# One tile of every fifth group fetched by SP, row by row, in a graph-network layer on one Trainium2 core

## The chip, the cores and the metric

The kernel runs on one core of one Trainium2 chip. The core has five engines that run their own instruction streams and meet through semaphores: TensorE (PE in the profile, with its weight loads shown as PEld), VectorE (DVE), ScalarE (ACT), GpSimd (POOL) and SyncE (SP), which computes nothing and issues transfers. Sixteen DMA engines move data between the chip's memory and the core's on-chip memory. SP and ACT issue transfers that hardware turns into descriptors; POOL issues gathers whose descriptors it makes itself, from a list of row numbers.

The metric is the device time of one execution in microseconds (us), as the median of several runs. A profiled execution gives the span from the first to the last instruction, and a record of each instruction.

## The reference

The kernel computes one layer of a graph network on 12500 nodes of 256 features, with 200000 edges sorted by destination. All is float32.

```python
h = jnp.maximum(_layernorm(x, axis=-1), 0.0)
agg = segment_sum(h[src], dst, num_segments=N)      # 200000 rows gathered and added up by node
z = (1.0 + eps_gin) * h + agg
t = relu(batchnorm(z @ W1 + b1, g1, bt1))           # 256 -> 512, statistics over all nodes
out = relu(batchnorm(t @ W2 + b2 + h, g2, bt2))     # 512 -> 256, statistics over all nodes
return x + out
```

The gather `h[src]` reads 200000 rows of 1 KB. Since a batch normalisation needs the statistics of all nodes, the kernel has three stages: everything up to `z @ W1`, then W2, then the output.

## The kernel before

**Tiles and groups.** The edges are cut into 1563 tiles of 128 edges (the last has 64), the tiles into 131 groups of 12 (`GT`). The nodes are cut into 25 chunks of 512. `srcT` holds the source node numbers, one column a tile; a gather of one tile fetches 128 rows, one to a partition.

**The first stage** is one loop over rounds i = 0 to 134 in `fast()` (L307), under `tc.manual_schedule()`: on each engine the instructions stand in the order in which the Python code records them. A round has, in this order:

- `gather(i + 4)` (L429): POOL issues 12 indirect transfers, tile 11 of the group first and tile 0 last, into the buffer of that group. There are five such buffers (`AHEAD + 1`), so a buffer is used again five groups later, once PE has read it. For the groups up to 29 (`LEAD`) the rows come from `x` and are normalised after landing (`settle`, L363); from group 30 on they come from `h_tab`, the table of normalised rows that the kernel itself wrote in rounds 0 to 24.
- `add` (L501) on DVE adds an earlier group's result into the chunk's accumulator `zc`.
- `take` (L522), when a slice is ready: DVE takes statistics (L525), ACT copies the slice to `ts` (L527) and stores it to `t_tab` (L528). A chunk has four slices, so there are about three `take`s in four rounds.
- `hold` (L483): ACT copies the sum of group i - 2 out of PSUM (`zs`, L485). `edges` (L460): DVE builds the selection matrices `oh` of group i + 1.
- `sums(i)` (L471): PE multiplies the 12 tiles by their selection matrices (L478), tile 0 first, and adds them up in one PSUM tile. Float32 matmuls appear as two records each, 24 to a group.
- `put(i - 2)` (L491): PE places the group's 128 sums at their nodes (L496).
- `z_load(c)` (L451): SP loads a chunk's `zc` start value from `h_cols` (four buffers); two rounds later `z_scale` (L458) on ACT scales it. `slice_of` (L509): PE computes one slice of `z @ W1` (L514).

**The second stage** loops over the chunks: SP loads `t_tab` (L626, three buffers) and `h_cols` (L627), ACT normalises (L630), PE multiplies by W2 (L637), DVE adds and takes statistics (L641, L642). **The third** normalises, transposes back, adds `x` and stores (L657 to L668). The order of these two is made by the framework's scheduler.

**Transfers and their counters.** The framework gives transfers that SP and ACT issue eight landing semaphores in turn, and a transfer waits until the one before it on the same semaphore has landed. POOL's gathers have eight of their own.

Of the kernel before, what the change touches and what calls it, by code (L numbers as in the profile page):

```python
# [6 lines left out]

F32 = mybir.dt.float32
I32 = mybir.dt.int32
AF = mybir.ActivationFunctionType  # L10
OP = mybir.AluOpType
PSUM = bass.MemoryType.PSUM
# [2 lines left out]
P = 128  # L15
R = 4
EPS = 1e-5
GT = 12
MARGIN = 64
AHEAD = 4  # L20
LEAD = 30
EARLY = 2
LOW = 8
XAHEAD = 10
XMORE = 6

# [7 lines left out]
def kernel(  # L34
# [16 lines left out]
    nc = tc.nc  # L51
    N, D = x.shape
# [9 lines left out]
    for g in range(NCH):  # L62
        rows = min(CH, N - g * CH)
# [9 lines left out]
    NG = -(-NTILE // GT)  # L73
# [7 lines left out]
    h_tab = dram.tile([N, D], F32, name="h_tab")  # L81

    def move(eng, sb, table, g, store):
# [13 lines left out]

    jp = consts.tile([P, P], I32, name="jp")
    nc.gpsimd.iota(jp, pattern=[[1, P]], base=0, channel_multiplier=-1)
# [6 lines left out]

    srcT = consts.tile([P, NBLK * P], I32, name="srcT")
    dstT = consts.tile([P, NBLK * P], F32, name="dstT")
    shift = consts.tile([P, NG], F32, name="shift")
    base = consts.tile([P, NG], F32, name="base")  # L110
    flag = consts.tile([1, 1], I32, name="flag")
    col_i = consts.tile([P, WIDE], I32, name="col_i")
    row_i = consts.tile([P, 1], I32, name="row_i")
    srcE = consts.tile([P, EARLY * GT], I32, name="srcE")
    lands = [
        (consts.tile([P, LOW, D], F32, name=f"gta{k}"), consts.tile([P, GT - LOW, D], F32, name=f"gtb{k}"))
        for k in range(EARLY)
    ]

    def slot(ga, t):  # L120

        if len(ga) == 1:
            return ga[0][:, t, :]
        return ga[0][:, t, :] if t < LOW else ga[1][:, t - LOW, :]

# [18 lines left out]
    at = 0  # L144
# [6 lines left out]
    with ExitStack() as es:  # L151
# [15 lines left out]
        with tc.issue_after(placed.ins):  # L167
# [35 lines left out]
            pb, lhsT=first, rhs=dstT[:, : NG * GT].rearrange("p (g t) -> p g t", t=GT)[:, :, 0],  # L203
            start=True, stop=True,
# [16 lines left out]
        below = raw.tile([P, NG * GT], F32, name="below")  # L221
# [11 lines left out]
        for k, (v, t0, rows, n, e) in enumerate(checks):  # L233
            nc.scalar.activation(
                below[:rows, :n], v[:rows, t0 : t0 + n], AF.Relu, bias=zero[:rows], scale=-1.0,
                accum_out=cnt[:rows, 2 * k : 2 * k + 1],
# [4 lines left out]
                op0=OP.add, op1=OP.max,  # L241
# [12 lines left out]
        at = 0  # L254
# [15 lines left out]
    def norm(pool, st, mv, count, gamma, beta, bias, tag):  # L270
# [6 lines left out]
        mean = pool.tile([P, count], F32, name="mean" + tag)  # L277
        nc.scalar.activation(sd, mv[:, :, 1], AF.Sqrt, bias=epst)
        nc.vector.reciprocal(sc, sd)
# [7 lines left out]
    def layernorm(ln, xt, w, ht):  # L287
# [6 lines left out]
        sd = ln.tile([P, R], F32, name="sd")  # L294
        nc.scalar.activation(sd[:w], mv[:w, :, 1], AF.Sqrt, bias=epst[:w])
        rs = ln.tile([P, R], F32, name="rs")
# [5 lines left out]
        for c in range(R):  # L302
            nc.scalar.activation(
                ht[:w, c, :], xt[:w, c, :], AF.Relu, bias=nb[:w, c : c + 1], scale=rs[:w, c : c + 1]
            )

    def fast():  # L307

        parts = []
        for n0, w in chunks:  # L310
            n = w * R
# [20 lines left out]
        with ExitStack() as fs:  # L332
            keep = fs.enter_context(tc.tile_pool(name="keep", bufs=1))
# [7 lines left out]
            with ExitStack() as es:  # L341
                ln = es.enter_context(tc.tile_pool(name="ln", bufs=2))
                gat = es.enter_context(tc.tile_pool(name="gat", bufs=AHEAD + 1 - EARLY))
                sel = es.enter_context(tc.tile_pool(name="sel", bufs=2))
# [18 lines left out]
                def settle(v, pairs, rows, to, tag):  # L363
# [4 lines left out]
                    for c in reversed(range(0, n, 2)):  # L368
                        two = v[0][:, c : c + 2, :] if len(v) == 1 or c < LOW else v[1][:, c - LOW : c - LOW + 2, :]
                        nc.vector.bn_stats(  # L370
# [3 lines left out]
                    sd = sel.tile([P, n], F32, name="sd" + tag)  # L374
                    nc.scalar.activation(sd, st[:, :, 2], AF.Sqrt, bias=epst, scale=1.0 / D)
                    rs = sel.tile([P, n], F32, name="rs" + tag)
# [3 lines left out]
                    for c in reversed(range(rows)):  # L380
                        nc.scalar.activation(  # L381
                            slot(to, c), slot(v, c), AF.Relu, bias=nb[:, c : c + 1], scale=rs[:, c : c + 1]
                        )

                xts, hts, pcs = {}, {}, {}

                def x_chunk(g):
# [41 lines left out]
                def gather(i):  # L429
                    t0, n = groups[i]  # L430
                    k = i % (AHEAD + 1)
                    ga = lands[k] if k < EARLY else (gat.tile([P, GT, D], F32, name="gt"),)
                    for t in reversed(range(t0, t0 + n)):
                        rows = left if t == full_tiles else P
                        nc.gpsimd.indirect_dma_start(  # L435
                            out=slot(ga, t - t0)[:rows], out_offset=None, in_=x if i < LEAD else h_tab,
                            in_offset=bass.IndirectOffsetOnAxis(ap=srcT[:rows, t : t + 1], axis=0),
                        )
                    gathered[i] = ga
# [31 lines left out]
                def sums(i):  # L471

                    t0, n = groups[i]
                    ga, oh = gathered.pop(i), ohs.pop(i)
                    ps = ps_s.tile([P, D], F32, name="ps")
                    for j in range(n):
                        rows = left if t0 + j == full_tiles else P
                        nc.tensor.matmul(  # L478
                            ps, lhsT=oh[:rows, j, :], rhs=slot(ga, j)[:rows], start=(j == 0), stop=(j == n - 1)
                        )  # L480
                    summed[i] = ps

# [47 lines left out]
                def first(c):  # L530

                    return min(i for i in range(NG) if c in reach(i))
# [6 lines left out]
                for i in range(EARLY, min(AHEAD, NG)):  # L539
                    gather(i)  # L540
# [3 lines left out]
                for c in range(NCH):  # L544
                    k = max(first(c) + 1, c + 2)
# [4 lines left out]
                for i in range(NG + 4):  # L550
                    before = added
                    if i + AHEAD < NG:
                        gather(i + AHEAD)

                    late = 4 if i < NG else 3
                    while added <= min(i - late, NG - 1):
                        add(added)
                        added += 1
                    for c, f in taken:
                        take(c, f)  # L560
                    taken = []
                    if 0 <= i - 2 < NG:
                        spots(i - 2)
                        hold(i - 2)
                    if i + 1 < NG:
                        edges(i + 1)

                    if i < NCH:
                        h_chunk(i)
                    if i + 1 < min(LEAD, NG):  # L570
                        settle(gathered[i + 1], GT // 2, GT, gathered[i + 1], "g")
                    for c in scales.get(i, ()):
                        z_scale(c)

                    if i < NG:
                        sums(i)
                    if 0 < i <= NCH:
                        turn(i - 1)
                        turn_out(i - 1)
                    if 0 <= i - 2 < NG:  # L580
                        put(i - 2)
                    for c in loads.get(i, ()):
                        z_load(c)
                    while whole < NCH and last(whole) < (before if i < NG else added):
                        queue += [(whole, f) for f in range(HC)]
                        whole += 1
                    if i < NG:
                        some = queue[:1]
                    else:
                        some = queue  # L590
                    queue = queue[len(some):]
                    if i < NG:
                        for c, f in some:
                            slice_of(c, f)
                        taken = some
                    else:
                        for c, f in some:
                            slice_of(c, f)
                            take(c, f)
# [7 lines left out]

            xin = fs.enter_context(tc.tile_pool(name="xin", bufs=XAHEAD - EARLY, reuse_waits="tile"))
            xrs = []

            def x_rows(g):
                if g < NCH:
                    if XAHEAD - EARLY <= g < XAHEAD:
                        xrs.append(lands[g - XAHEAD + EARLY][1])
                    else:
                        pool = xmore if XAHEAD <= g < XAHEAD + XMORE else xin
                        xrs.append(pool.tile([P, R, D], F32, name="xr"))
# [3 lines left out]
            with tc.tile_pool(name="tin", bufs=3, side="right", reuse_waits="tile") as tin, tc.tile_pool(name="ps_y", bufs=4, space=PSUM) as ps_y:  # L621

                for k, g in enumerate([*range(NCH - 2), NCH - 1, NCH - 2]):
                    n = chunks[g][1] * R
# [9 lines left out]
                    for d in range(DC):  # L634
                        py = ps_y.tile([P, CH], F32, name="py")
                        for f in range(HC):
                            nc.tensor.matmul(  # L637
                                py[:, :n], lhsT=w2s[:, f, d * P : (d + 1) * P], rhs=tT[:, f, :n],
                                start=(f == 0), stop=(f == HC - 1),
                            )  # L640
                        nc.vector.tensor_add(yT[g][:, d, :], py[:, :n], yT[g][:, d, :])  # L641
                        nc.vector.bn_stats(st2[:, d, g, :], yT[g][:, d, :])  # L642
                for g in range(XAHEAD):
                    x_rows(g)
# [4 lines left out]
            with tc.tile_pool(name="xmore", bufs=XMORE, side="right", reuse_waits="tile") as xmore, tc.tile_pool(  # L649
                name="ps_o", bufs=3, space=PSUM  # L650
            ) as ps_o:
                for g in range(XAHEAD, XAHEAD + XMORE):
                    x_rows(g)
# [270 lines left out]
```

## Time and profile before

| | us |
|---|---|
| median of 3 runs (lowest to highest) | 2235.57 (2233.42 to 2241.05) |
| the profiled execution's own time | 2235.88 |
| its span | 2233.7 |
| POOL's last gather ends at | 1959.3 |
| PE's last matmul of L478 ends at | 1970.9 |

| engine | busy us | share of the span |
|---|---|---|
| PE | 1478.6 | 66% |
| POOL | 1480.4 | 66% |
| DVE | 716.5 | 32% |
| ACT | 510.1 | 23% |

How to read the profile: busy time does not count the instructions that only issue a transfer, wait, branch or load a register, so SP has no busy time at all and its issues are listed under SPq (ACT's under ACTq). A line such as `1204.72 0.94 POOL L435 DMA_INDIRECT gt<-h_tab,srcT x1 [0.30 <-issue]` is the start, the duration, the engine, the source line, the operation, what is written and read, how many instructions are merged, and in brackets how long the engine sat idle before it and what ended that; "issue" means that it waited for nothing that the profile shows. In the windows by engine the columns are PE, PEld, DVE, ACT and POOL, each with busy time and number of instructions. DMA shares are means over 16 engines. The five gather buffers are named gt, gta and gtb (two are split in two).

### The profile page before, as it was taken

How to read it: one execution, taken by the hardware profiler on the slowest of the kernel's cores; microseconds unless marked ns; L12 is line 12 of the kernel's file. 1: busy time of each engine (PE TensorE's matmuls, PEld its weight loads, DVE VectorE, ACT ScalarE, POOL GpSimd, SP SyncE). 2: the span in 40 equal slices, each digit the busy share in tenths (PEclk: the TensorE clock that was granted, in tenths of full speed). 3: DMA queues.
4: the chain of work that ended last, by engine and by line, in shares of the span. 5: the costliest groups of instructions: out<-in, count | busy, mean ns of one | idle time of the engine just before them, and what ended most of it. 6: DMA issues, size and time to landing. Idle time of an engine off the chain costs nothing.

```text
span 2233.7 us, 15142 instructions
## 1 busy us (share of the span) xinstructions
PE 1478.6 (66%) x4874; PEld 1066.5 (48%) x4874; DVE 716.5 (32%) x1092; ACT 510.1 (23%) x963; POOL 1480.4 (66%) x1575
## 2 busy tenths in 40 slices
PE   3567677667666666656666666666666666679994
PEld 2455545545444544544454444444444544444443
DVE  5566656531222122122212221211221121124345
ACT  4666666520000000000000000000000000034445
POOL 7777777777777777777777777777777777700000
PEclk9888888888888788878877887888887788789998
DMA  6677767644444444444444444444443444438739
GB/s 196 208 228 232 246 218 237 183 128 120 129 128 129 116 128 129 120 123 129 131 116 125 132 120 125 129 117 126 129 133 113 126 128 118 130 131 320 252 118 311
DMA packets 157615, 349.47 MB, mean 156 GB/s; under 512 B 30104, under 2 KB 82452, under 8 KB 154454
## 3 DMA queue, kind: packets, MB, share of 16 engines
q0 software_dynamic: 75008, 204.90, 32.8%
q1 hardware_dynamic: 54224, 104.03, 13.9%
q10 hardware_dynamic: 28294, 39.47, 4.9%
q8 instruction: 41, 0.67, 0.1%
q14 instruction: 48, 0.39, 0.1%
HBM read 284.28 MB, written 64.00 MB: 156 GB/s over the span
## 4 chain that ended last, share of the span: by engine, by line
POOL 52%; issue 22%; PE 11%; ACT 6%; DVE 4%; DMA 4%; ACTq 0%; SPq 0%; DVEq 0%; POOLq 0%
POOL gt L435 32%; POOL gta L435 12%; PE py L637 8%; POOL gtb L435 6%; DMA gt<-in_x_dram,srcT 3%; ACT gt L381 2%; DVE stg L370 2%; PE ps L478 2%; PE ph L514 1%; ACT yT L657 1%; ACT gta L381 1%; DMA out_dram<-xr 1%; DVE oh L464 1%; POOL gta L212 1%; ACT gtb L381 0%
## 5 line engine op out<-in xcount | busy, mean ns | idle before, releaser
L478 PE MATMUL ps<-gt,oh 128*128 128x256 f32 x1872 | 577.0, 481 | 402.5 <-DMA gt<-h_tab,srcT 321.5
L435 POOL DMA_INDIRECT gt<-h_tab,srcT x720 | 680.7, 945 | 219.3 <-issue 219.3
L478 PEld LDWEIGHTS ps<-gt,oh 128*128 128x128 f32 x1872 | 459.1, 250 | 546.0 <-issue 315.7
L478 PE MATMUL ps<-gta,oh 128*128 128x256 f32 x838 | 291.9, 524 | 270.5 <-DMA gta<-h_tab,srcT 212.1
L478 PEld LDWEIGHTS ps<-gta,oh 128*128 128x128 f32 x838 | 224.8, 275 | 352.4 <-issue 198.3
L525 DVE BATCH_NORM_STATS2 st<-ph 128x6 f32<-128x512 f32 (+1 forms) x100 | 68.4, 684 | 971.2 <-PE ph L514 971.2
L435 POOL DMA_INDIRECT gta<-h_tab,srcT x323 | 305.2, 945 | 98.4 <-issue 95.9
L527 ACT COPY ts<-ph 128x512 f32<-128x512 f32 (+1 forms) x100 | 57.4, 574 | 1326.5 <-DVE st L525 1326.5
L435 POOL DMA_INDIRECT gt<-in_x_dram,srcT x216 | 204.2, 945 | 65.8 <-issue 60.9
L464 DVE TENSOR_TENSOR oh<-col,dstT 128x1536 f32<-128x1536 f32 x131 | 227.7, 1738 | 0.0
L514 PE MATMUL ph<-zc,w1s 128*128 128x512 f32 (+1 forms) x400 | 193.1, 610 | 20.6 <-DVE hc L423 20.1
L507 DVE TENSOR_TENSOR zc<-pz,zc 128x512 f32<-128x512 f32 (+8 forms) x187 | 93.9, 520 | 282.5 <-PE pz L496 244.2
L435 POOL DMA_INDIRECT gtb<-h_tab,srcT x160 | 151.2, 945 | 48.7 <-issue 47.5
L637 PE MATMUL py<-gta,w2s 128*128 128x512 f32 (+1 forms) x400 | 169.6, 587 | 3.7 <-ACT gta L630 3.7
L496 PE MATMUL pz<-at,zs 128*128 128x256 f32 x524 | 134.9, 380 | 5.0 <-ACT zs L485 5.0
L637 PEld LDWEIGHTS py<-gta,w2s 128*128 128x128 f32 x400 | 76.4, 192 | 96.4 <-issue 75.7
L514 PEld LDWEIGHTS ph<-zc,w1s 128*128 128x128 f32 x400 | 78.3, 199 | 79.8 <-issue 49.1
L381 ACT ACTIVATE gt<-gt,nbg,rsg 128x256 f32<-128x256 f32 x216 | 108.1, 586 | 9.1 <-DVE nbg L379 8.1
L496 PEld LDWEIGHTS pz<-at,zs 128*128 128x128 f32 x524 | 97.6, 190 | 19.1 <-ACT zs L485 7.1
L630 ACT ACTIVATE gta<-ti,of,sc 128x512 f32<-128x512 f32 (+1 forms) x100 | 79.6, 803 | 82.9 <-PE py L637 78.8
L478 PE MATMUL ps<-gtb,oh 128*128 128x256 f32 x416 | 98.3, 379 | 0.0
L435 POOL DMA_INDIRECT gta<-in_x_dram,srcT x80 | 75.6, 946 | 24.4 <-issue 8.5
(97 smaller groups left out, 897.3 us busy)
## 6 DMA issues: line engine op xcount, KB each, us to landing
t_tab<-ts ACTq DMA_DIRECT2D x96, 256.0 KB
ti<-t_tab SPq DMA_DIRECT2D x24, 1024.0 KB
xt<-in_x_dram SPq DMA_DIRECT2D x24, 512.0 KB
h_tab<-ht ACTq DMA_DIRECT2D x24, 512.0 KB
h_cols<-hc SPq DMA_DIRECT2D x24, 512.0 KB
zc<-h_cols SPq DMA_DIRECT2D x24, 512.0 KB
yT<-h_cols SPq DMA_DIRECT2D x24, 512.0 KB
gt<-h_tab,srcT POOLq DMA_INDIRECT x720, 2.8
```

The source lines that it names most:

```text
L370: nc.vector.bn_stats(st[:, c : c + 2, :].rearrange("p c s -> p (c s)"), two.rearrange("p c d -> p d c"),)
L381: nc.scalar.activation(slot(to, c), slot(v, c), AF.Relu, bias=nb[:, c : c + 1], scale=rs[:, c : c + 1])
L435: nc.gpsimd.indirect_dma_start(out=slot(ga, t - t0)[:rows], out_offset=None, in_=x if i < LEAD else h_tab, in_offset=bass.IndirectOffsetOn ...
L464: nc.vector.tensor_tensor(ohs[i][:, :n, :], col[:, :P].unsqueeze(1).to_broadcast([P, n, P]), dstT[:, t0 : t0 + n].unsqueeze(2).to_broadcas ...
L478: nc.tensor.matmul(ps, lhsT=oh[:rows, j, :], rhs=slot(ga, j)[:rows], start=(j == 0), stop=(j == n - 1))
L496: nc.tensor.matmul(pz[:, d, :], lhsT=zs[:, d * P : (d + 1) * P], rhs=at, start=True, stop=True)
L507: nc.vector.tensor_add(side, pz[:, :, a - lo : b - lo], side)
L514: nc.tensor.matmul(ph[:, :n], lhsT=w1s[:, d, f * P : (f + 1) * P], rhs=zc[c][:, d, :n], start=(d == 0), stop=(d == DC - 1),)
L525: nc.vector.bn_stats(st1[:, f, c, :], ph[:, :n])
L527: nc.scalar.copy(ts[:, :n], ph[:, :n])
L630: nc.scalar.activation(tT[:, f, :n], ti[:, f, :n], AF.Relu, bias=of1[:, f : f + 1], scale=sc1[:, f : f + 1],)
L637: nc.tensor.matmul(py[:, :n], lhsT=w2s[:, f, d * P : (d + 1) * P], rhs=tT[:, f, :n], start=(f == 0), stop=(f == HC - 1),)
```

## The change

In the 19 groups 34, 39, ... 124 (`by_row`), `gather` leaves out tile 0, so POOL issues 11 gathers and not 12. The 128 rows of that tile are fetched by SP into a tile of their own, `one` (three buffers), and `sums` reads `one` for j = 0 of these groups.

A row's address is its node number times 1024 bytes. ACT loads the 19 x 128 node numbers once at the start of the stage (`rows_i`), DVE multiplies them (`rows_b`). For 16 rows at a time SP then loads 16 addresses into registers with one instruction and issues 16 transfers of 1 x 1024 bytes from `h_tab`, each with its source address in a register. Two such batches are recorded a round, ahead of the rest of the round, so the eight batches of group G are recorded in rounds G - 8 to G - 5.

```diff
+APART = 5
+BATCH = 16
...
+                by_row = range(LEAD + 4, NG - 6, APART)
+                rows_i = keep.tile([len(by_row), P], I32, name="rows_i")
+                nc.scalar.dma_start(rows_i, ...)
+                rows_b = keep.tile([len(by_row), P], I32, name="rows_b")
+                nc.vector.tensor_scalar(rows_b, rows_i, float(4 * D), None, op0=OP.mult)
+                h_bytes = h_tab.rearrange("n d -> (n d)").bitcast(U8)
+                single, pending = {}, []
+
+                def begin_rows(k):
+                    i = by_row[k]
+                    single[i] = sel.tile([P, D], F32, name="one", bufs=3)
+                    pending.extend((k, b) for b in range(0, P, BATCH))
+
+                def some_rows(count):
+
+                    for _ in range(min(count, len(pending))):
+                        k, b = pending.pop(0)
+                        to = single[by_row[k]]
+                        _, at = nc.values_load_multi_w_load_instructions(
+                            rows_b[k : k + 1, b : b + BATCH], engines=[mybir.EngineType.SP], min_val=0,
+                            max_val=(N - 1) * 4 * D,
+                            skip_runtime_bounds_check_because="node numbers are below N",
+                        )
+                        for q, v in enumerate(at):
+                            nc.sync.dma_start(
+                                to[b + q : b + q + 1, :].bitcast(U8),
+                                h_bytes[bass.ds(v, 4 * D)].rearrange("(o e) -> o e", o=1),
+                            )
...
-                    for t in reversed(range(t0, t0 + n)):
+                    for t in reversed(range(t0 + (i in by_row), t0 + n)):
...
+                    alone = single.pop(i, None)
...
-                            ps, lhsT=oh[:rows, j, :], rhs=slot(ga, j)[:rows], start=(j == 0), stop=(j == n - 1)
+                            ps, lhsT=oh[:rows, j, :], rhs=alone if alone is not None and j == 0 else slot(ga, j)[:rows], start=(j == 0), stop=(j == n - 1)
...
                     if i + AHEAD < NG:
                         gather(i + AHEAD)
+                    if i + APART + 3 in by_row:
+                        begin_rows(by_row.index(i + APART + 3))
+                    some_rows(2)
```

More of the change, by code (lines that the diff above doesn't have):

```diff
@@ L9 @@
 I32 = mybir.dt.int32
+U8 = mybir.dt.uint8
 AF = mybir.ActivationFunctionType
@@ L383, in settle @@
                         )
+                by_row = range(LEAD + 4, NG - 6, APART)
+                rows_i = keep.tile([len(by_row), P], I32, name="rows_i")
+                nc.scalar.dma_start(
+                    rows_i,
+                    bass.AP(
+                        tensor=src.tensor, offset=src.offset + by_row[0] * GT * P,
+                        ap=[[APART * GT * P, len(by_row)], [1, P]],
+                    ),
+                )
[20 more added lines that the diff above has]
+                                h_bytes[bass.ds(v, 4 * D)].rearrange("(o e) -> o e", o=1),
+                            )
                 xts, hts, pcs = {}, {}, {}
```

## The prediction

> **What bounds the kernel now.** I read four things in this order: the busy shares and slices (who is busy all the time, and when), the chain of work that ended last (does that engine carry the end), that engine's own timeline (is it waiting for anybody), and what SP's queue is doing meanwhile, since it gets the work.
>
> The page, busy shares and two lines of the slices:
>
> ```profile
> PE 1478.6 (66%) x4874; PEld 1066.5 (48%) x4874; DVE 716.5 (32%) x1092; ACT 510.1 (23%) x963; POOL 1480.4 (66%) x1575
> ...
> POOL 7777777777777777777777777777777777700000
> ...
> POOL 52%; issue 22%; PE 11%; ACT 6%; DVE 4%; DMA 4%; ACTq 0%; SPq 0%; DVEq 0%; POOLq 0%
> ```
>
> PE and POOL have the same share, 66%. POOL's is the same "7" in every slice up to 1959 us and the chain lies on it: 52% POOL and 22% "issue", which are one thing, as its timeline shows (start, duration, idle before it):
>
> ```profile
> 514.70 0.95 POOL L435 DMA_INDIRECT gt<-h_tab,srcT  x1 [0.30 <-issue]
> 515.95 0.95 POOL L435 DMA_INDIRECT gt<-h_tab,srcT  x1 [0.30 <-issue]
> 517.20 0.95 POOL L435 DMA_INDIRECT gt<-h_tab,srcT  x1 [0.30 <-issue]
> ```
>
> One gather of 128 rows every 1.25 us (0.95 + 0.30), 12 to a group, 15.0 us a group. POOL's waits from 516 to 1959 us say that it waits for nobody:
>
> ```profile
> POOL gt L435 <- issue: 212.0, 696, 0.3
> POOL gta L435 <- issue: 93.5, 307, 0.3
> POOL gtb L435 <- issue: 46.3, 152, 0.3
> ```
>
> No buffer, landing or engine is in that list. PE does wait for POOL, here for one group's first tile:
>
> ```profile
> 1204.72 0.94 POOL L435 DMA_INDIRECT gt<-h_tab,srcT  x1 [0.30 <-issue]
> ...
> 1207.86 7.68 PEld L478 LDWEIGHTS ps<-gt,oh 128*128 128x128 f32 x24 [5.25 <-issue]
> 1207.89 8.06 PE L478 MATMUL ps<-gt,oh 128*128 128x256 f32 x24 [4.88 <-DMA gt<-h_tab,srcT]
> ```
>
> And the stretch by engine (last numbers: granted PE clock, busy share of the 16 DMA engines, GB/s):
>
> ```profile
> 1200.00:1959.00 759.00, 480.23 (x1563) 363.66 (x1563) 160.75 (x209) 48.80 (x96) 574.12 (x608) 0.81 0.44 125
> 1959.00:2234.00 275.00, 230.20 (x686) 119.41 (x686) 114.36 (x164) 122.18 (x167) 0.26 (x1) 0.92 0.65 227
> ```
>
> POOL's 574.12 us busy are 608 gathers at 1.25 us pitch = 760 us: the whole stretch. PE has 37% of it free, DMA 56%, ACT 94%. After 1959 us a tail of 275 us follows, on PE and ACT, without POOL. So whatever is taken off POOL's count of gathers comes off the time, while the others keep up.
>
> **The change, part by part.**
>
> *Removed.* The groups 34, 39, ... 124 are 19; each loses the gather of its tile 0, the last POOL issues for it. 19 x 1.25 = **-23.75 us**. Five groups take 5 x 15.0 - 1.25 = **73.75 us** instead of 75.
>
> *Added on SP's queue.* Per such group 8 register loads and 128 transfers of one row; 19 x 128 = 2432 transfers. The trace has no transfer with an address in a register. The nearest rows are SP's one-piece loads, a register load, and SP's loads of 128 partitions (ns: min/median/max):
>
> ```profile
> L175 SPq DMA_DIRECT2D rawi_s<-in_src_dram x2: 251/255/259, 8.7 to 9.0; - x2
> ...
> L889 SPq TENSOR_LOAD <-flag x1: 467/467/467, 25.7 to 25.7; - x1
> ...
> L330 SPq DMA_DIRECT2D xt<-in_x_dram x26: 332/434/783, 26.6 to 351.0; - x26
> ```
>
> The two L175 loads, one contiguous piece each as a row is, together take 0.56 us in SP's timeline, gap included: 0.28 us each, my lower end. The median of xt with that gap (0.56 - 2 x 0.255 = 0.05) is 0.48, my upper end. I take 0.35: near the one-piece rows, with 0.07 for the register and its bound. A tile then costs 128 x 0.35 + 8 x (0.467 + 0.05) = 44.8 + 4.1 = **48.9 us** of SP (ends 39.9 and 65.6) in the 73.75 us that it has: hidden, 0 on the path. What hides it: SP has next to nothing else there; its largest wait is for a free zc buffer:
>
> ```profile
> SPq L454 <- PE ph L514: 1384.5, 18, 89.3
> ```
>
> If that cover is gone: it is, when a row costs over (73.75 - 4.1) / 128 = **0.544 us**. From there each 0.01 us more costs 24.3 us over the 2432 rows, less a reserve: the group above ends on PE at 1216, and POOL needs its buffer again only when it starts group +5, four groups after 1205.9, at 1265.9, so about 50 us may be lost once before POOL waits.
>
> *Are the rows there in time?* Rows of group G go out in rounds G-8 to G-5, two batches of 16 a round, so the last is five rounds (74 us) before the matmul. A round's batches take SP 2 x (16 x 0.35 + 0.52) = 12.2 of 15 us. One gather lands 2.8 us after its issue (page, transfers). Cost 0; lateness would first show as PE waiting for "one".
>
> *Queues that the rows are put into.* (a) SP is in order: zc loads now stand behind rows. Before, SP stood ready at the wait above, up to 89 us early; now a zc load goes out at most some 13 us into its round, and its reader, ACT's scaling L458, comes two rounds (30 us) later; behind it waits DVE's addition into zc. Hidden; without that cover ACT, then DVE and PE, would be late, each against the same 50 us. (b) SP and ACT take turns on eight landing counters, as the built program's waits show: each transfer waits until the eighth before it has landed. So at most eight rows are in flight. The first load of the program was issued at 0.75 and its reader started at 2.59, 1.84 us; 1.84 / 8 = 0.23 us a row, 2.8 / 8 = 0.35: not above what I took for the issue. (c) ACT's t_tab store gets a place in that turn too, so ACT now waits for a row, and a row for the store; what is behind the store on ACT is zs (L485), for which PE's L496 waits. The loop from one store to the next: landing 2.8, then 17 rows at 0.35 = 6.0, a register load 0.5, landing 2.8, issue 0.3 = 12.4 us in a round of 14.75. Cost 0; at 0.48 a row 14.6, just inside. (d) POOL's own queue only gets shorter.
>
> *DMA engines.* The same bytes in smaller pieces. SP's packets average 13.9% x 16 x 2233.7 / 54224 = 0.092 us; 32 a round on one engine, if a row stays in one piece there, is 2.9 us of 14.75 and takes that engine from 0.44 to about 0.64. Cost 0 to POOL, which has not waited for a landing.
>
> *Start.* One more load on ACT at 26.7 us (0.27 to 0.57 us, as the vrows loads; ACT then idles 6.59 us until DVE's L370) and one small DVE operation (0.15 to 0.28 us) that waits for it until about 26.7 + 1.84 = 28.5; DVE reaches it at 28.8. 0 on the path, as POOL is in its 1.25 us pitch since 4.6 us; at worst 0.6. PE's wait for 128 rows is a few more semaphore instructions in a gap of 4.88 us: 0.
>
> *Tail.* SP's order there changes a little: three t_tab loads that alternated with three h_cols loads now follow them. Each still waits for ACT to free its buffer ("SPq L626 <- ACT gta L630", 22 times). 0; ends -2 and +2, from three issues of 0.43 us and what they displace.
>
> *A rule against it.* The Trainium skill (DMA: Bandwidth & Descriptors, Anatomy of one DMA and Rules for kernel authors) gives about 2.0 us fixed for each transfer and says that under 64 KB one pays mostly overhead. By it, if nothing overlapped, 128 rows would be about 256 us a tile, an estimate from that page; the L175 pair, 0.30 us apart without waiting for a landing, speaks for overlap. The same page (Issuing engines are not separate DMA queues) says that issuing from several engines saves only issue time, usually small beside the transfer; here issue time is the bound, 1.25 us with DMA at 0.44, so its condition is not met.
>
> **Sum.** The profiled execution took 2235.88 us (span 2233.7 and 2.2 around it; the median of the runs, 2235.57, is 0.3 lower). 2235.88 - 23.75 + 0 = **2212.1 us**, 1.06% faster.
>
> **The rivals.**
>
> *SP becomes the bound (slower).* Place: the row transfers on SP's queue. Price: a register address that makes a row dear, say 0.65 us. Then 128 x 0.65 + 4.1 = 87.3 us a tile, 13.6 over budget, 19 x 13.6 = 258, less the 50 in reserve = 208: 2212 + 208 = 2420 us. It is slower than before only from 0.544 + (50 + 23.75) / 2432 = 0.574 us. For it: no register transfer in the trace, and single xt loads up to 0.783. Against: those carry 512 KB, a row 1 KB, and the one-piece rows are 0.25. Chance 0.10.
>
> *Rows do not overlap (slower).* Should the in-flight eight land one after another, a row costs its landing, 1.84 us: 128 x 1.84 + 4.1 = 240 us a tile, 19 x 166 - 50 = 3100 more, about 5300 us. For it only that all rows may share one DMA engine. Chance 0.02; that is the case of the Trainium skill's fixed cost above.
>
> *The gain is eaten on ACT (no change).* At 0.53 a row the loop of (c) is 15.5 us and exceeds the round by 0.7; 72 stores in the stretch make 50 us, the reserve, and jitter then costs POOL about what it gained: 2235 us. For it: ACT's order is rigid. Against: ACT is 6% busy. Chance 0.04.
>
> **How the numbers follow.** Forecast 0.84. A measurement of this kernel tells no change from one of 0.3% (6.7 us; the three runs span 7.6). Faster 0.84, same 0.04, slower 0.10 + 0.02 = 0.12. The range holds the forecast alone, as 0.84 is enough: 2212 less 2 for the tail and 4 for the runs' spread below, 2206; above 2 for the tail, 0.6 for the start and some 7 for the runs' high side (2241 against a median of 2235.6), 2222.
>
> **What would show it.** Right: POOL's 1.25 us pitch unchanged and 19 gathers fewer, its last at about 1935; SP's rows at 0.28 to 0.48 us; PE's first matmuls of those groups no later than the others. Wrong: rows over 0.54 us; PE waiting for "one"; POOL waiting for PE (a buffer) in the later groups; ACT waiting before t_tab; a tail longer than 275 us.

## The result, and the profile after

The changed kernel takes 2212.70 us (median of 4 runs, 2211.28 to 2213.55), the kernel before 2235.53 us beside it (2233.42 to 2241.05): a ratio of 0.9896, 95% interval 0.9881 to 0.9912. The profiled execution took 2212.03 us, span 2210.0. The forecast was 2212.1 (2206 to 2222).

In the changed kernel the lines move: the gather L435 is L473, PE's sums L478 are L517, `zs` L485 is L524, the slice L514 is L553, `zc`'s load and scaling L454 and L458 are L492 and L496, the store of `t_tab` L528 is L567. New are the row transfers, L418, and their register loads, L412.

The page of the changed kernel, busy shares, POOL's slices and the chain:

```profile
PE 1388.4 (63%) x4874; PEld 1005.3 (45%) x4874; DVE 716.0 (32%) x1093; ACT 511.3 (23%) x963; POOL 1463.2 (66%) x1556
...
POOL 7777777777777777777777777777777777700000
...
POOL 39%; issue 18%; PE 17%; DMA 8%; SPq 7%; ACT 7%; DVE 3%; ACTq 0%; DVEq 0%; POOLq 0%
```

POOL is as even as before, with 19 instructions fewer (1556 against 1575). But the chain now leaves POOL: SPq, which had 0%, holds 7%, PE 17% instead of 11%, DMA 8% instead of 4%. A chain is followed back from the last instruction to whatever released each one, so a share on it is no proof of a cost; here it says that around the rows something comes as late as POOL does. POOL's own waits from 516 to 1937 us tell whether it loses by that:

```profile
POOL gt L473 <- issue: 205.4, 674, 0.3
POOL gta L473 <- issue: 93.6, 307, 0.3
POOL gtb L473 <- issue: 45.7, 150, 0.3
```

It does not: only its own 0.3 us between gathers (the other lines of that answer are single gaps of the same 0.3 us). The stretches by engine (PE, PEld, DVE, ACT, POOL; granted clock, DMA share, GB/s) confirm the pace:

```profile
1200.00:1937.00 737.00, 434.09 (x1562) 331.69 (x1562) 161.70 (x210) 49.70 (x96) 557.29 (x590) 0.79 0.46 129
1937.00:2210.00 273.00, 228.41 (x683) 117.79 (x682) 114.30 (x164) 122.16 (x167) 0.00 (x0) 0.93 0.65 228
```

590 gathers in 737 us are 1.25 us each, as before; the last one ends at 1936.8 instead of 1959.3 us, and the tail is 273 us instead of 275. DMA goes from 0.44 to 0.46.

So much is as forecast. SP's queue is not. The rows by source line (duration in ns, min/median/max), and the register loads:

```profile
L418 SPq MOVE one<-h_tab x2432: 29/29/38, 425.4 to 1868.0; - x188
L418 SPq DMA_DIRECT2D one<-h_tab x2432: 221/228/323, 425.5 to 1868.0; - x188
```

```profile
L412 SPq TENSOR_LOAD <-rows_b x152: 1160/1248/1509, 423.8 to 1859.0; - x152
```

A row is two instructions, one that moves the address and one that issues; the median distance between two rows is 0.323 us. A register load of 16 addresses takes 1.25 us. A tile is then 128 x 0.323 + 8 x 1.28 = 51.6 us of issuing (1.28 is a load with the gap behind it). Yet from its first register load to its last row a tile occupies SP for 75.8 us on average; the other 24 us are waiting. The first tile is much the worst: it takes 120 us, from 423.8 to 543.8, so its last row goes out when POOL has already issued the group's last gather. The 18 tiles after it take 73.6 us each (the last row ends at 1868.3), POOL's own pace for five groups: SP does not fall further behind, but it does not catch up for long either. What SP and the others wait for, from 500 to 1850 us (two answers, SP's queue first):

```profile
SPq L418 <- DMA t_tab<-ts: 380.4, 64, 23.6
```

```profile
DVE zc L546 <- ACT zc L496: 662.9, 17, 48.4
ACT zc L496 <- DMA zc<-h_cols: 661.9, 17, 48.2
...
PE pz L535 <- ACT zs L524: 281.4, 17, 24.7
...
PE ps L517 <- DMA one<-h_tab: 135.7, 9, 24.1
```

A row waits for a store that ACT issued; ACT waits for a `zc` load that SP issued, and DVE for ACT; PE waits for ACT and for rows. In the kernel before none of them is in ACT's and PE's lists from 516 to 1959 us, here whole:

```profile
ACT ts L527 <- DVE st L525: 1249.2, 72, 33.3
ACT zs L485 <- PE ps L478: 66.9, 6, 12.3
ACT zs L485 <- ACT ts L527: 29.2, 72, 0.7
```

```profile
PE ps L478 <- DMA gt<-h_tab,srcT: 315.5, 58, 7.3
PE ps L478 <- DMA gta<-h_tab,srcT: 205.7, 38, 7.2
PE ps L478 <- DVE zc L507: 3.5, 1, 3.5
```

Together the new waits make PE late. In the kernel before PE began a group, from group 31 on, 1.9 to 3.8 us after the group's own last gather had been issued; now it is up to 29.3 us (group 100). From PE's last sum of a group to POOL's next use of its buffer there were 48 to 53 us; now the least is 24.1 us. The reserve was half used, and since it was not all used POOL never waited and the time shows nothing.

One case, group 99 (rows of the fourteenth tile). The timeline of the changed kernel from 1455 to 1480 us, all engines, of which ACT's copy and store and SP's next rows are shown, and then PE's from 1480 us:

```profile
1458.54 0.58 ACT L566 COPY ts<-ph 128x512 f32<-128x512 f32 x1 [23.74 <-DVE st L564]
...
1459.15 0.33 ACTq L567 DMA_DIRECT2D t_tab<-ts  x1
...
1462.19 17.84 SPq L418 DMA_DIRECT2D one<-h_tab  x15
```

```profile
1509.49 1.19 PE L517 MATMUL ps<-one,oh 128*128 128x256 f32 x2 [24.15 <-DMA one<-h_tab]
```

SP had issued row 45 of the tile at 1442.5; the next row goes out 19.7 us later. ACT issues the store at 1459.15; 3.0 us later, when it has landed, row 46 goes out and eight more follow, and then SP waits 12 us again, for the store that ACT issues at 1475.78. (The 18 us of the SP line are these 9 rows, that wait and 6 rows more.) The tile's last row goes out at 1507.4. POOL had issued the group's last gather by 1489.2; PE starts 20.3 us after that.

### The profile page after: what moved, and what is told of

It reads as the page before. It is cut to its first block, busy times and chain, and to the rows that moved or that the text cites. A ratio compares the mean times of both kernels' runs of the same rounds, so it can differ in the third digit from the quotient of the medians.

```text
span 2210.0 us, 20247 instructions
## 1 busy us (share of the span) xinstructions
PE 1388.4 (63%) x4874; PEld 1005.3 (45%) x4874; DVE 716.0 (32%) x1093; ACT 511.3 (23%) x963; POOL 1463.2 (66%) x1556
## 4 chain that ended last, share of the span: by engine, by line
POOL 39%; issue 18%; PE 17%; DMA 8%; SPq 7%; ACT 7%; DVE 3%; ACTq 0%; DVEq 0%; POOLq 0%
POOL gt L473 24%; POOL gta L473 9%; PE py L679 8%; PE ps L517 5%; SPq L418 5%; POOL gtb L473 5%; DMA gt<-in_x_dram,srcT 3%; PE ph L553 2%; ACT gt L384 2%; SPq L412 1%; PE pz L535 1%; ACT yT L699 1%; DVE stg L373 1%; DMA t_tab<-ts 1%; DMA gta<-in_x_dram,srcT 1%
## 5 line engine op out<-in xcount | busy, mean ns | idle before, releaser
L473 POOL DMA_INDIRECT gt<-h_tab,srcT x701 | 662.6, 945 | 213.6 <-issue 212.1
L517 PE MATMUL ps<-gt,oh 128*128 128x256 f32 x1834 | 497.1, 436 | 185.6 <-DMA gt<-h_tab,srcT 104.3
L517 PEld LDWEIGHTS ps<-gt,oh 128*128 128x128 f32 x1834 | 407.0, 224 | 290.7 <-issue 110.1
L473 POOL DMA_INDIRECT gta<-h_tab,srcT x323 | 305.3, 945 | 98.5 <-issue 96.9
L535 PE MATMUL pz<-at,zs 128*128 128x256 f32 x524 | 152.7, 418 | 286.4 <-ACT zs L524 286.4
L517 PE MATMUL ps<-gta,oh 128*128 128x256 f32 x838 | 241.7, 452 | 135.6 <-DMA gta<-h_tab,srcT 73.0
L517 PEld LDWEIGHTS ps<-gta,oh 128*128 128x128 f32 x838 | 192.7, 234 | 197.5 <-issue 91.2
L473 POOL DMA_INDIRECT gt<-in_x_dram,srcT x216 | 204.1, 945 | 65.8 <-issue 61.8
L553 PE MATMUL ph<-zc,w1s 128*128 128x512 f32 (+1 forms) x400 | 207.5, 649 | 11.6 <-DVE hc L461 10.9
L496 ACT ACTIVATE zc<-zc,gin 128x1024 f32<-128x1024 f32 (+1 forms) x25 | 28.1, 1124 | 672.4 <-DMA zc<-h_cols 672.4
L473 POOL DMA_INDIRECT gtb<-h_tab,srcT x160 | 151.2, 945 | 48.8 <-issue 47.8
L553 PEld LDWEIGHTS ph<-zc,w1s 128*128 128x128 f32 x400 | 85.9, 217 | 80.2 <-issue 56.2
L517 PE MATMUL ps<-one,oh 128*128 128x256 f32 x38 | 17.4, 551 | 146.1 <-DMA one<-h_tab 146.1
```

What stands on the lines that cost most here:

```text
L473: nc.gpsimd.indirect_dma_start(out=slot(ga, t - t0)[:rows], out_offset=None, in_=x if i < LEAD else h_tab, in_offset=bass.IndirectOffsetOn ...
L517: nc.tensor.matmul(ps, lhsT=oh[:rows, j, :], rhs=alone if alone is not None and j == 0 else slot(ga, j)[:rows], start=(j == 0), stop=(j == ...
L535: nc.tensor.matmul(pz[:, d, :], lhsT=zs[:, d * P : (d + 1) * P], rhs=at, start=True, stop=True)
L553: nc.tensor.matmul(ph[:, :n], lhsT=w1s[:, d, f * P : (f + 1) * P], rhs=zc[c][:, d, :n], start=(d == 0), stop=(d == DC - 1),)
```

## Experiments

Five kernels, each with one or two things changed, tell what the waits are. Each ratio is to the kernel before, run on the same chip in the same set.

**1. No tile 0 at all.** The 19 tiles are neither gathered nor fetched; PE adds 11 tiles in those groups, and the output lacks their edges.

```diff
-                    for j in range(n):
+                    j0 = 1 if i in by_row else 0
+                    for j in range(j0, n):
...
-                            ps, lhsT=oh[:rows, j, :], rhs=alone if alone is not None and j == 0 else slot(ga, j)[:rows], start=(j == 0), stop=(j == n - 1)
+                            ps, lhsT=oh[:rows, j, :], rhs=slot(ga, j)[:rows], start=(j == j0), stop=(j == n - 1)
...
-                    if i + APART + 3 in by_row:
-                        begin_rows(by_row.index(i + APART + 3))
-                    some_rows(2)
```

> In the 19 groups tile 0 is left out altogether: POOL does not gather it, SP fetches no rows, PE sums 11 tiles (so these sums lack 128 edges each, and PE has 38 matmul records fewer). If the whole gain is POOL's 19 gathers and SP's rows cost nothing, the time is that of the change: 2212 us, between 2209 and 2215. If the rows and what they delay take back a part of the gain, this one is faster than the change by that part: below 2209. PE's waits for ACT and ACT's waits for zc (281 and 672 us with the change) should both be near those of before.

Measured: 2212.76 us (2211.20 to 2215.22), ratio 0.9902 (0.9886 to 0.9919), the time of the changed kernel. So the rows cost the time nothing, and the whole gain is POOL's 19 gathers. Of ACT's waits from 500 to 1850 us this answer is left:

```profile
ACT ts L567 <- DVE st L565: 1184.4, 69, 32.5
ACT zs L525 <- PE ps L518: 57.3, 5, 12.5
ACT zs L525 <- ACT ts L567: 27.4, 69, 0.4
```

No wait for `zc`: the 662 us come with the rows. (ACT's long wait before `ts` is its idle time; a slice comes only when PE has one.)

**2. The `zc` loads on ACT's queue**, so that they no longer stand behind rows.

```diff
-                    nc.sync.dma_start(zc[c][:, :, :n], h_cols[c, :, :, :n])
+                    nc.scalar.dma_start(zc[c][:, :, :n], h_cols[c, :, :, :n])
```

> The change, with the loads of zc issued by ACT in place of SP, so that they no longer stand behind rows. If the wait of ACT for zc comes from SP's queue, it falls from 672 us to under 100 us, SP's wait for t_tab stores (390 us) falls with it, and PE's latest start after its group's last gather falls from 29 us to under 15. The time: if the reserve of the gather buffers had absorbed the delay, 2212 us as with the change (2209 to 2215); if the delay had cost time, below 2209.

Measured: 2212.39 us (2210.97 to 2213.49), ratio 0.9895 (0.9879 to 0.9912). ACT's wait for `zc` is gone. The lateness is not, against what was expected: PE's latest start after a group's last gather is now 33.8 us, not under 15. SP and PE, from 500 to 1850 us:

```profile
SPq L418 <- DMA t_tab<-ts: 385.3, 61, 23.6
```

```profile
PE ps L517 <- DMA one<-h_tab: 568.8, 18, 36.2
```

SP waits for `t_tab` as long as before (385.3 against 380.4), PE's 135.7 us for `one` have become 568.8, and the least distance to POOL's reuse falls from 24.1 to 18.3 us. The late `zc` load was a consequence: SP was standing at a row, with the load behind it. That leaves SP's wait for `t_tab` as the cause; experiment 4 changes it.

**3. Every fourth group, 23 tiles.** Here POOL leaves SP 47 x 1.25 = 58.75 us for a tile, more than the 51.6 us that it needs to issue one. Since rows begin `APART + 3` rounds ahead, they are also recorded one round later, in rounds G - 7 to G - 4.

```diff
-APART = 5
+APART = 4
```

> The change for every fourth group, 23 in place of 19. POOL alone: 2235.9 - 23 x 1.25 = 2207 us. SP's issues for a tile, 128 x 0.32 + 8 x 1.28 = 51.5 us, fit into 4 x 15 - 1.25 = 58.75 us, so if SP's issue time is all that matters, 2207. If SP and ACT hold each other up (rows wait for t_tab stores, ACT waits for zc loads behind rows: 390 and 672 us with the change), the tile takes more than 58.75 us and the lateness grows past the reserve of about 50 us: above 2212, up to some 2300.

Measured: 2343.05 us (2340.20 to 2345.04), ratio 1.0477 (1.0460 to 1.0495); once more, on another chip:

> Every fourth group with the old turn, as the run at 2343 us, on the same chip as the kernel with the new turn. Theory of the turn: slower than that one by some 130 us (2343 us where the kernel before takes 2235 us), SP's waits for t_tab about 296 us. Rival (SP's own issue): within 20 us of it.

2345.70 us (2341.53 to 2349.67), ratio 1.0491 (1.0473 to 1.0508). In this second run a tile occupies SP for 68.6 us on average, though its row pitch is still 0.323 us: 119 us for the first, and 66.4 us for each of the 22 after it (the last row ends at 2006.3 us). SP's and POOL's waits, 500 to 1850 us:

```profile
SPq L418 <- DMA t_tab<-ts: 292.4, 59, 25.1
```

```profile
POOL gt L473 <- PE ps L517: 82.7, 13, 9.5
...
POOL gtb L473 <- PE ps L517: 37.1, 7, 9.5
```

POOL now waits for PE's sums. The tiles after the first fall behind POOL's pace by 66.4 - 58.75 = 7.7 us each until the reserve is used up (0.3 us is left at the least), and from then on POOL pays: in this stretch 119.8 us in 20 waits of at most 9.5 us, over the whole run 143.5 us in 24. With the `zc` loads on ACT as well it is no better:

> Every fourth group, and the loads of zc issued by ACT. If the kernel with every fourth group alone is late because of the zc loads behind the rows, this one is at POOL's count again: 2207 us (2204 to 2210). If it is late because of SP's own issue time or the turn of the landing counters with ACT's stores, this one is as late as that.

2373.42 us (2370.73 to 2377.93), ratio 1.0624 (1.0607 to 1.0642). So `zc` is not it, in this kernel either.

**4. The turn of the landing counters.** SP and ACT share eight landing semaphores; a transfer waits for the one that had its semaphore before. Which store a row stands behind is settled when the program is built, and can be read off the built program. A row is recorded in one of four rounds (G - 8 to G - 5 in the changed kernel, G - 7 to G - 4 in the two others), a store in the round of its `take`. Counted from the two kernels' programs, and from the third one that is described next:

```
                                     changed   every fourth   every fourth
                                     kernel    group          group, new turn
rows that stand behind a store           76         74             71
  a store of 2 or more rounds later      69         69              0
  than the row's own round
  a store of the group's own round       39         58              0
  or of the three rounds before it
```

In the changed kernel seven rows stand behind a store of the very round in which PE needs them. Row 46 of the case above is recorded in round 92 and stands behind the store of round 97. So the rows are not sent in the rounds in which they are recorded, eight to five ahead, but as ACT's stores get done, and those come from PE's slices: PE, ACT and SP wait for each other round by round, with two landings in the loop. Why the framework deals the semaphores out in this order the program does not say; the order is what counts here.

The edit makes the store wait for the row before the newest batch, so that a store stands behind the rows of its own round and a row never behind a later round's store. The transfers, their queues and the rounds of the rows stay as in experiment 3; ACT's store gets one more thing to wait for.

```diff
-APART = 5
+APART = 4
...
+                            row = nc.sync.dma_start(...)
+                        newest.append(row)
...
+                    store = nc.scalar.dma_start(t_tab[c, :, f, :n], ts[:, :n])
+                    if len(newest) > 1:
+                        tc.add_manual_dep(
+                            store.ins, newest[-2].ins.name,
+                            mybir.DependencyInfo(mybir.DependencyClass.Sync, mybir.DependencyReason.DATA),
+                            reason="turn",
+                        )
```

> Every fourth group with the new turn of the landing counters, beside every fourth group with the old turn on the same chip. Theory (the old turn ties SP's rows to ACT's stores of t_tab): this kernel is faster than the one with the old turn, by some 130 us where the kernel before takes its 2235 us (2203 to 2212 us against 2343), and SP's waits for t_tab are below 150 us. Rival (SP's queue can't fetch 128 rows in 58.75 us, whatever the turn): no more than 20 us between the two.

Measured, on the same chip and in the same set as the second run of experiment 3: **2206.81 us** (2204.56 to 2208.98), ratio 0.9866 (0.9849 to 0.9882), against 2345.70 with the old turn. The difference, 139 us, is about what POOL waited there, 143.5 us, and the time is the 2235.5 - 23 x 1.25 = 2206.8 of the theory. SP's, POOL's and ACT's waits, 500 to 1850 us:

```profile
SPq L418 <- DMA t_tab<-ts: 100.4, 61, 4.1
```

```profile
POOL gt L474 <- issue: 197.5, 648, 0.3
```

```profile
ACT ts L567 <- DVE st L565: 1117.8, 69, 35.5
ACT zs L525 <- DMA one<-h_tab: 100.4, 37, 9.7
ACT zs L525 <- PE ps L518: 31.1, 5, 8.5
```

SP still waits at 61 rows, but 4.1 us at most instead of 25.1. Its tiles follow each other every 58.5 us, POOL's own pace, and the first takes 64.5 us instead of 119. POOL waits for nobody (gta and gtb show the same 0.3 us). PE begins a group at most 3.8 us after its last gather, as in the kernel before, and from group 34 on at least 47 us lie between PE's last sum and the reuse. ACT's wait for `zc` is gone too, with the `zc` loads still behind the rows on SP. What is new is ACT's wait for a row, 100.4 us in 37 pieces, the price of the edit, and it is hidden. 128 rows in 58.75 us are no problem for SP; the turn was. This kernel is the fastest of all that ran. The changed kernel itself, at every fifth group, was not run with the new turn on a chip where the kernel before takes its 2235 us.

**5. Other chips.** Six runs fell on three chips on which the kernel before itself took 2530 to 2543 us, and they can't be set beside the others. Rows fetched and the gather kept (expected at the time of the kernel before):

> POOL gathers tile 0 of the 19 groups too (the first matmuls of the group still take the rows that SP fetched, and what POOL gathered for that tile is not used). Theory (POOL's 19 gathers are the whole difference, the rows cost nothing): the time of the kernel before, 2235.5 us (2232 to 2240). Rival (the gain comes from something else, a moved buffer or the start): 2212 to 2225 us.

3010.57 us against 2530.16, ratio 1.1911 (1.1874 to 1.1948). The changed kernel with the new turn:

> The changed kernel with the same new turn of the landing counters. Theory: POOL stays the bound, so the time stays at 2212 us (2209 to 2215); what changes is the reserve: SP's waits for t_tab fall from 385 us to below 150 us, and the least slack between PE's end of a group's sums and POOL's reuse of the buffers rises from 24 us to above 35 us. Rival (SP's waits for t_tab come from the stores' own lateness, not from the turn): waits and slack as they were.

2758.55 us, ratio 1.0908 (1.0867 to 1.0949). Every fourth group with the new turn, on two of these chips:

> Every fourth group as in the run at 2343 us, 23 tiles, the same transfers on the same queues; only the order changes in which the row transfers and the 100 stores of t_tab take the eight landing counters: each store of t_tab is made to wait for the row before the newest batch recorded so far, so that it stands behind the rows of its own round and no row stands behind a store of a round later than its own (before, rows of a group stood behind stores of up to the group's own round, the very round that needs them). Theory (the turn of the landing counters ties SP to ACT's t_tab stores, and SP's own issue, 51.5 us of each 58.75 us, fits): the loss goes, 2235.5 - 23 x 1.25 = 2206.8 us, between 2203 and 2212; SP's waits for t_tab fall from 296 us to below 150 us, PE's wait for the row tile from 246 us to below 100 us, POOL waits for no sums. Rival (128 rows a tile are too much for SP's queue at this pace, whatever the turn): 2330 to 2350 us, with POOL waiting for PE's sums as before.

> The same kernel as in the run of every fourth group with the new turn of the landing counters, because in that set the kernel before itself took 2530 us. Where the kernel before takes its 2235 us: theory (the turn ties SP to ACT's stores of t_tab) 2206.8 us, between 2203 and 2212, SP's waits for t_tab below 150 us, no wait of POOL for PE's sums; rival (128 rows a tile are too much for SP's queue at every fourth group) 2330 to 2350 us.

2894.81 and 2909.66 us, ratios 1.1457 (1.1419 to 1.1495) and 1.1435 (1.1388 to 1.1482). Every third group, 31 tiles, with three batches of rows a round in place of two, meant to let SP's own issue become the bound, on two of them as well:

> Every third group, 31 tiles, with the new turn; POOL would take 43.75 us for three groups less one gather. Theory (one tile costs SP 128 x 0.322 + 8 x 1.28 = 51.5 us, and now nothing else ties it): SP becomes the bound by its issue, 31 x 51.5 = 1597 us from the first row at about 424 us to the last at about 2020 us, and the end some 300 to 340 us later: 2320 to 2365 us; SP waits little and POOL waits for PE's sums. Rival (the rows overlap more than their pitch says, or POOL stays the bound): 2235.5 - 31 x 1.25 = 2197 us.

> Every third group, 31 tiles, with the new turn of the landing counters, so that only SP's own issue is left to hold the rows: POOL's pace leaves 43.75 us for a tile, the row pitch of 0.322 us and eight register loads of 1.25 us make 51.5 us. Theory (SP now becomes the bound): mean distance of two tiles on SP 51 to 55 us, the last row at about 424 + 31 x 52 = 2036 us, POOL's last gather some 15 to 30 us later, and 273 us of tail: 2315 to 2350 us. Rival (POOL stays the bound): 2235.5 - 31 x 1.25 = 2196.8 us.

3244.78 and 3264.88 us, ratios 1.2838 (1.2796 to 1.2880) and 1.2820 (1.2773 to 1.2868). None of the times was met, on either theory. SP's waits for `t_tab` did go where the turn was new (7.9 us in all from 500 to 1900 us in the changed kernel with the new turn), but the rows were late all the same. What the records show is that instructions which wait for nothing take long. The run of the changed kernel with the new turn, POOL's timeline in the stretch before any row is fetched, and the row transfers by source line:

```profile
169.79 0.95 POOL L474 DMA_INDIRECT gt<-in_x_dram,srcT  x1 [0.30 <-issue]
175.64 0.94 POOL L474 DMA_INDIRECT gtb<-in_x_dram,srcT  x1 [4.89 <-ACT hc L460]
```

```profile
L418 SPq MOVE one<-h_tab x2432: 1/29/1402, 544.4 to 2371.5; - x188
L418 SPq DMA_DIRECT2D one<-h_tab x2432: 1/228/1399, 545.9 to 2372.9; - x188
```

The medians are the old ones, 29 and 228 ns, but a register move takes up to 1402 ns where it took 38 at most; 466 of the 2432 moves take over 100 ns, 285 us in all, and 339 of these last 0.65 to 0.75 us. POOL shows one such hole of 4.9 us between early gathers about every 35 us (the engine named behind it is only the last one seen). A tile then occupies SP for 96.0 us on average, more than the 73.75 that POOL's undisturbed pace leaves. That fits a disturbance that can hit any instruction and a change that gives SP thousands of them, but what holds the instructions was not found. No more code was loaded there: one of the two instruction queues (q14) carried 87 packets in this run and 88 in the changed kernel as it is, the other (q8) 41 in both. The changed kernel as it is did not run on those chips, so whether it still gains there is open; so are the time with rows fetched and the gather kept on the other chips, and the pace at which SP's own issue would bound on the others.

## Why the prediction was right, point by point

**POOL bounds, 19 gathers fewer: right.** -23.75 forecast, -23.85 between the two profiled executions; pitch 1.25 kept, last gather at 1936.8 (forecast about 1935). Experiment 1, without these gathers and without rows, takes the same time, so the rows cost nothing here.

**A tile on SP, 48.9 us: measured 51.6 of issuing, with one term wrong.** The row was nearly right: 0.323 us against 0.35. The register load was priced by the row of a load of one value, 0.467 us; 16 values in one instruction take 1.25 us. On 8 loads this is 6.2 us a tile; it stays within 73.75.

**"Are the rows there in time?": the step that failed.** It said that the last rows go out five rounds before the matmul because they are recorded there. They go out as the counters' turn lets them: in group 99 the last row goes out 18 us after POOL has issued the group's last gather. The cost on the time, 0, came out, but the 74 us of lead did not exist. Two of its own signs of failure are in the profile: PE waits for "one", and PE's first matmuls of such groups come late, in group 99 20.3 us after the last gather, against at most 3.8 in the kernel before.

**(c), the shared turn: seen, and wrongly costed.** The loop of 12.4 us in a round of 14.75 supposed that a store stands among the rows of its own round. It stands among rows recorded up to six rounds earlier, so the loop runs through PE's sums as well. Cost 0 on the path, but 423 us of waiting on SP over the whole run, and the next step of the same change (experiment 3) turns it into 139 us of time. With the order that (c) supposed (experiment 4) the waits are short and the step holds.

**(a), `zc` loads hidden: wrong about the wait, right about the time.** ACT waits 672 us for them over the whole run, up to 48.2 at once. The cover of 30 us was worked out for a load behind 13 us of rows, not behind a row that waits for a store.

**(b) and the Trainium skill's fixed cost.** Eight rows in flight are enough: in the stretch from 500 to 1850 us rows make SP wait for rows 2.0 us in all. The Trainium skill (DMA: Bandwidth & Descriptors, Anatomy of one DMA) gives about 2.0 us fixed for each transfer, and gives it for transfers that GpSimd issues, while the rows are SP's. A time of that order shows here in a landing (in group 99, 3.0 us from the issue of the 256 KB store to the row behind it), not in the pitch of rows, 0.323 us: they overlap, and the 256 us a tile that it would give without that did not come.

**The reserve of about 50 us** is what made the forecast come true although the steps on the rows' arrival, (c) and (a) went wrong. It was counted above all as a cover for a dear row and served as a cover for the turn; 24.1 us of it were left. That it was enough is luck: the prediction had put this wait at 0, and with every fourth group (experiment 3) it was not enough.

**Start, tail, DMA:** the first 330 gathers take 414 us in both; tail 273 against 275, inside its 2 us; DMA 0.46. **The rivals:** none came, but the first, SP late and POOL waiting, is what experiment 3 shows, not by a dear row but by the turn. In the rival on ACT the loop at 0.53 us a row adds up to 15.4 us, not 15.5; nothing hangs on that.

## What to carry to other kernels

Where two queues share landing counters in turn, look in the built program at which transfer stands behind which: moving many small transfers onto a queue can tie it to another engine's late stores, and recording them early did not help here. Before taking such a change a step further, read how much of the buffers' reserve is left (here 24 of 50 us, with no sign of it in the time). And measure on more than one chip: thousands of added instructions on an idle queue are free only as long as they run at their usual pace.

## What the hardware showed that was not expected

- A register load of 16 values takes SP 1.25 us, one of a single value 0.467.
- A transfer of 1 KB with its address in a register is issued in 228 ns, plus 29 ns for moving the address; the pitch is 0.323 us.
- On three chips plain register moves took up to 1.4 us (38 ns at most elsewhere), and on the first of them gathers had holes of 4.9 us without a wait; the kernel before took 13% longer there (2530.16 us against 2235.53), every fourth group with the new turn 31% longer (2894.81 against 2206.81).
